# Where the sums of the two left-over keys stand in a unit's chain of sums: cross-attention and state-space kernel on one core

## The chip, the cores and the metric

The kernel runs on one core of one Trainium2 chip. The metric is the device time of one execution in microseconds (us), given as the median of the runs. The engines are TensorE (PE in the profile, its weight loads PEld), VectorE (DVE), ScalarE (ACT), GpSimd (POOL) and SyncE (SP, which issues DMAs).

## What is computed

The reference is one block of a sequence model, in float32, with batch 1, 4096 queries, 3202 keys, width 512, 8 heads of 64:

```
x  = layernorm(builder_state);  base_n = layernorm(base_state)      # 4096 x 512, 3202 x 512
x  = residual + mha(x, base_n)                                      # softmax attention, 8 heads
U  = (layernorm(x) @ W_in.T + b_in) @ Bmat                          # 4096 x 64
s  = silu(s @ A.T) + u_t   for t = 0 .. 4095                        # the scan
out = x + states @ Cmat + mean(program_probs) @ W_prog.T + b_prog
```

Softmax needs, for each query, the sum over 3202 keys of exp(score). The change concerns the order in which the parts of that sum are added up.

## The kernel before

**Preparation.** The keys and values are projected and written to DRAM, in chunks of 256 keys (12 chunks of 256, then one of 128: 3200 keys, `NDC` = 13 chunks with `c` = 0 to 12). The two keys that are left over (`REST` = 2) stay in SBUF tiles `kx` and `vx`.

**Units.** The attention runs over 64 units, numbered `i` = 0 to 63. A unit is a block of 512 queries (`Q` = 0 to 7), a pair of heads (`hp` = 0 to 3) and a half of the block's queries (`half`, 256 queries); the eight units of a block are 8Q to 8Q + 7. Each unit has, for each chunk `c`:

- `("scores", i, c)` on PE, line 635: eight matmuls of 64x256 into one of two PSUM tiles (ring `s`).
- `("weights", i, c)` on ACT, line 705: the exponential, 128x1024, into a tile `p`.
- `("product", i, c)` on PE, line 745: the weights times the values, accumulated in PSUM tile `po`. There is one `po` (ring `o`), so `("product", i, 0)` has to wait for `("join", i - 1)`.
- `("add", i, c)` for `c` = 1 to 12, line 713: a chain, the sum of the weights of all chunks into `acc`. The sums with `c` in `POOL_SUMS = (2, 6, 10)` run on POOL, the others on DVE. In the last unit all of them run on DVE.
- `("rest", i)` on DVE, line 699: two small sums that add the weights of the two left-over keys (tile `extra`) into rows of `acc`, on 2 partitions x 256 elements each.

After the last chunk come `("output", i)` (ACT, line 780: a copy of half of `po`), `("join", i)` (DVE, line 784: the other half of `po` added to it, which frees `po`), `("fold", i)` (POOL, line 720), `("sums", i)` (PE, line 763), `den` (ACT), `whole`, `inverse`, `scale` and `fall` (DVE, lines 801 to 811).

**Other work between the units.** Once in a half block PE has the output projection `("rows", Q, half, "outs")` of the block before (line 988, 16 matmuls of 128x512), and four times in a block the query projection `("heads", Q + 1, hp)` of the next block (line 312).

**The order.** Every one of these steps is a piece with an engine, an estimated cost, a due time, the pieces that it comes after, and slots of rings that it takes and gives back (`plan.add`). `Plan.order` (line 100) plays the pieces through with the estimated costs, each engine taking the ready piece that is due first, and the order that comes out is the order in which the instructions of every engine are written. On the chip each engine runs its instructions in that order and waits for semaphores. A changed dependence or cost of one piece therefore also changes the order of others.

In the chain of sums, `before` names the piece that a sum follows, and the `rest` piece is put in after `add` 1:

```python
before = {1: ("weights", i, 0), 2: ("rest", i)}.get(c, ("add", i, c - 1))
...
if c == 1:
    plan.add(("rest", i), "DVE", 1200, partial(rest, w), [("add", i, 1), ("extra", first)],
```

The chain of a unit is thus add 1 (DVE), rest (DVE), add 2 (POOL), add 3, 4, 5 (DVE), add 6 (POOL), add 7, 8, 9 (DVE), add 10 (POOL), add 11, 12 (DVE).

## Time and profile before

| | |
|---|---|
| time, median of 3 runs | 2006.42 us (2005.42 to 2007.58) |
| the profiled execution: its time | 2004.45 us |
| the profiled execution: span in the trace | 2002.6 us |
| PE busy | 1954.1 us (98%) |
| DVE busy | 1259.4 us (63%) |
| ACT busy | 1130.1 us (56%) |
| POOL busy | 789.5 us (39%) |
| mean granted PE clock | 0.995 |

A row of costly groups reads: line, engine, operation, output <- inputs, shapes, count, then total busy time and the mean time of one in ns, then the idle time of the engine just before these instructions and what ended it. A row of the waits reads: who waited, for whom, the total in us, how many times, the longest. A row of the timeline reads: start, duration, engine, line, operation, tiles, shape, count of the instructions that are merged in it, and in brackets the idle time before and its releaser. The row "windows" gives the busy time of engines in a stretch and the granted PE clock in it.

### The profile page before, as it was taken

The numbers are of one execution on the slowest core, as the hardware profiler recorded it, in microseconds if no ns is written. First come the engines' busy times: TensorE is split into PE (matmuls) and PEld (weight loads), VectorE is DVE, ScalarE is ACT, GpSimd is POOL, SyncE is SP. The second block draws the span as 40 slices with busy tenths as digits, with TensorE's granted clock in tenths as the row PEclk, the third lists the DMA queues.
The fourth block names the chain that finished last, engine by engine and source line by source line (L and its number), as shares of the span: only waits on it lengthen the run. The fifth ranks groups of instructions, "written<-read, shape, count | busy, mean of one in ns | idle before, by whom it ended". The sixth has DMA issues, their size and how long they took to land. (4 is left out here: it accounts for less than half of the span.)

```text
span 2002.6 us, 66617 instructions
## 1 busy us (share of the span) xinstructions
PE 1954.1 (98%) x29070; PEld 1251.4 (62%) x29070; DVE 1259.4 (63%) x1533; ACT 1130.1 (56%) x1478; POOL 789.5 (39%) x631
## 2 busy tenths in 40 slices
PE   8999999999999999999999999999999999999996
PEld 4444566666666666666666666666666666666764
DVE  4311367566866677667756785667766675667575
ACT  2233466566666566556656665666565666655552
POOL 2111234345533454245434543445334642444424
PEclk9999999999999999999999999999999999999998
DMA  5632323224332243123322332234322331444485
GB/s 173 192 100 66 101 80 97 58 79 111 106 79 79 82 112 92 59 81 90 107 65 79 106 107 73 79 95 113 86 78 59 101 92 52 148 142 144 129 207 182
DMA packets 246934, 204.28 MB, mean 102 GB/s; under 512 B 80808, under 2 KB 220072, under 8 KB 246636
## 3 DMA queue, kind: packets, MB, share of 16 engines
q1 hardware_dynamic: 242088, 192.28, 33.4%
q10 hardware_dynamic: 4548, 7.67, 1.2%
q8 instruction: 231, 3.78, 0.8%
q14 instruction: 67, 0.55, 0.1%
HBM read 156.32 MB, written 29.88 MB: 93 GB/s over the span
## 5 line engine op out<-in xcount | busy, mean ns | idle before, releaser
L705 ACT ACTIVATE p<-s,shifts 128x1024 f32<-128x1024 f32 (+1 forms) x832 | 883.2, 1080 | 559.7 <-PE s L635 540.0
L745 PE MATMUL po<-p,v 64*64 64x256 f32 x12800 | 822.6, 377 | 10.6 <-DVE o L784 10.6
L635 PE MATMUL s<-q,k 64*64 64x256 f32 x12800 | 826.5, 377 | 4.9 <-ACT p L705 3.9
L713 DVE TENSOR_TENSOR acc<-p,acc 128x1024 f32<-128x1024 f32 (+1 forms) x515 | 633.3, 1230 | 249.0 <-POOL acc L713 179.4
L713 POOL TENSOR_TENSOR acc<-p,acc 128x1024 f32<-128x1024 f32 x189 | 449.2, 2376 | 679.1 <-ACT p L705 362.2
L635 PEld LDWEIGHTS s<-q,k 64*64 64x64 f32 x12800 | 482.6, 133 | 233.3 <-ACT p L705 32.5
L745 PEld LDWEIGHTS po<-p,v 64*64 64x64 f32 x12800 | 487.8, 133 | 209.7 <-DVE o L784 15.2
L720 POOL TENSOR_TENSOR acc<-acc 128x512 f32<-128x512 f32 x64 | 91.5, 1430 | 160.9 <-DVE acc L713 153.3
L713 DVE TENSOR_TENSOR acc<-p,p 128x1024 f32<-128x1024 f32 x64 | 99.5, 1555 | 75.8 <-ACT p L705 70.2
L312 PE MATMUL pq<-xn,wq 128*128 128x512 f32 x256 | 118.3, 605 | 0.0
L804 DVE RECIPROCAL rd<-rd 128x256 f32<-128x256 f32 (+1 forms) x65 | 112.4, 1729 | 2.2
L988 PE MATMUL pa<-wo,o 128*128 128x512 f32 x240 | 107.0, 599 | 0.0
L699 DVE TENSOR_TENSOR acc<-x,acc 2x256 f32<-2x256 f32 x128 | 95.2, 744 | 2.5
L551 PE MATMUL pv<-wv,ct 128*128 128x512 f32 (+1 forms) x208 | 95.5, 611 | 1.0 <-ACT ct L519 0.7
L584 PE MATMUL pk<-ct,wk 128*128 128x512 f32 (+1 forms) x224 | 88.8, 549 | 0.0
L312 PEld LDWEIGHTS pq<-xn,wq 128*128 128x128 f32 x256 | 46.0, 189 | 57.6 <-issue 57.5
L784 DVE TENSOR_TENSOR o<-po,o 128x256 f32<-128x256 f32 x64 | 27.1, 423 | 84.3 <-ACT o L780 83.7
L988 PEld LDWEIGHTS pa<-wo,o 128*128 128x128 f32 x240 | 44.4, 190 | 56.0 <-issue 53.7
L321 ACT ACTIVATE q<-pq,bias 128x512 f32<-128x512 f32 x32 | 22.0, 687 | 98.4 <-PE pq L312 98.4
L519 DVE COPY ct<-tp_c 128x512 f32<-128x512 f32 (+1 forms) x13 | 8.5, 651 | 104.1 <-PE tp_c L283 104.1
L584 PEld LDWEIGHTS pk<-ct,wk 128*128 128x128 f32 x224 | 39.2, 190 | 42.6 <-issue 42.6
L551 PEld LDWEIGHTS pv<-wv,ct 128*128 128x128 f32 (+1 forms) x208 | 38.1, 192 | 44.3 <-issue 42.1
(215 smaller groups left out, 1200.3 us busy)
## 6 DMA issues: line engine op xcount, KB each, us to landing
k<-kd SPq DMA_DIRECT2D x432, 128.0 KB, 2.2
v<-vd SPq DMA_DIRECT2D x432, 128.0 KB, 2.3
xn<-x SPq DMA_DIRECT2D x416, 32.0 KB, 1.9
xr<-in_x_dram SPq DMA_DIRECT2D x30, 256.0 KB, 3.7
x1d<-xr SPq DMA_DIRECT2D x30, 256.0 KB, 3.4
x<-in_x_dram SPq DMA_DIRECT2D x28, 256.0 KB, 3.2
cx<-in_ctx_dram SPq DMA_DIRECT2D x25, 256.0 KB, 2.9
vd<-vs SPq DMA_DIRECT2D x25, 256.0 KB, 2.4
```

The costliest lines, as they stand in the source:

```text
L312: nc.tensor.matmul(pq, wq[:, i, hp * P : (hp + 1) * P], xn[:, i, :], start=(i == 0), stop=(i == NC - 1),)
L551: nc.tensor.matmul(pv[h * HD : h * HD + n, :H], ct[:, k, o : o + n], wv[:, k, :], start=(i == 0), stop=(i == NC // parts - 1), skip_group_ ...
L584: nc.tensor.matmul(pk[:, :n_g], wk[:, i, hp * P : (hp + 1) * P], ct[:, i, :n_g], start=(i == 0), stop=(i == NC - 1),)
L635: nc.tensor.matmul(s[k0 : k0 + HD, a, b, :], kts[(*w["at"][:2], c)][r, b * CK + k0 : b * CK + k0 + HD], q[r], start=True, stop=True, skip_ ...
L699: nc.vector.tensor_tensor(to[r], t[r], to[r], ALU.add)
L705: nc.scalar.activation(t[:, :, :nb, :], w["ps"][c][:, :, :nb, :], AF.Exp, bias=w["shift"])
L713: engine.tensor_tensor(w["acc"][:, :, :nb, :], t[:, :, :nb, :], before[:, :, :nb, :], ALU.add)
L720: nc.gpsimd.tensor_tensor(acc[:, :, 0, :], acc[:, :, 0, :], acc[:, :, 1, :], ALU.add)
L745: nc.tensor.matmul(w["po"][a * HD : (a + 1) * HD, k, :QU], vts[Q, hp, c][r, b, a * HD : (a + 1) * HD], t[r, a, b, :], start=(c == 0 and b ...
L784: nc.vector.tensor_tensor(o, rows_of(w, w["po"][:, 1, :QU], True), o, ALU.add)
L804: nc.vector.reciprocal(w["rd"][:, part], w["rd"][:, part])
L988: nc.tensor.matmul(v["pa"], o_t[Q, c, half][:, t * P : (t + 1) * P], wo[:, c, :], start=(c == 0), stop=(c == NC - 1),)
```

## The change

The two small sums stand after add 4 and before add 5, add 2 follows add 1 directly, and the planner's estimated cost of the `rest` piece is 900 ns in place of 1200 ns. The instructions are the same ones.

```diff
             if c:
                 dve = w["last"] or c not in POOL_SUMS
-                before = {1: ("weights", i, 0), 2: ("rest", i)}.get(c, ("add", i, c - 1))
+                before = {1: ("weights", i, 0), 5: ("rest", i)}.get(c, ("add", i, c - 1))
                 plan.add(("add", i, c), "DVE" if dve else "POOL", (100 + 1200 * part) if dve else 2382,
                          partial(add, w, c, nc.vector if dve else nc.gpsimd),
                          [("weights", i, c), before], d + 1200,
...
-            if c == 1:
-                plan.add(("rest", i), "DVE", 1200, partial(rest, w), [("add", i, 1), ("extra", first)],
+            if c == 4:
+                plan.add(("rest", i), "DVE", 900, partial(rest, w), [("add", i, 4), ("extra", first)],
                          d + 1300, [], [("extra", ("extra", first))])
```

## The prediction

> **What bounds the kernel now.** I read the page first, for the bound and the price of the moved work.

> ```profile
> PE 1954.1 (98%) x29070; PEld 1251.4 (62%) x29070; DVE 1259.4 (63%) x1533; ACT 1130.1 (56%) x1478; POOL 789.5 (39%) x631
> ...
> L699 DVE TENSOR_TENSOR acc<-x,acc 2x256 f32<-2x256 f32 x128 | 95.2, 744 | 2.5
> L784 DVE TENSOR_TENSOR o<-po,o 128x256 f32<-128x256 f32 x64 | 27.1, 423 | 84.3 <-ACT o L780 83.7
> ```

> PE is the bound; a small sum costs nothing by itself, whether it lies early or late, unless PE ends up waiting. The waits of PE say where that is. Its longest is for the join (L784), the one reader that frees the single `po`:

> ```profile
> PE po L745 <- DVE o L784: 10.6, 8, 2.6
> ```

> So I followed, unit by unit, the DVE queue ahead of each join in the timeline. Between units 10 and 11 the join is late, yet PE loses nothing:

> ```profile
> 506.43 2.63 DVE L713 TENSOR_TENSOR acc<-p,p 128x1024 f32<-128x1024 f32 x1 [0.96 <-ACT p L705]
> ...
> 508.98 1.94 DVE L713 TENSOR_TENSOR acc<-p,acc 128x1024 f32<-128x1024 f32 x2
> 509.14 1.91 PE L635 MATMUL s<-q,k 64*64 64x256 f32 x32
> ...
> 510.83 1.82 DVE L699 TENSOR_TENSOR acc<-x,acc 2x256 f32<-2x256 f32 x2
> ...
> 510.97 7.13 PE L988 MATMUL pa<-wo,o 128*128 128x512 f32 x16
> ...
> 512.68 0.42 DVE L784 TENSOR_TENSOR o<-po,o 128x256 f32<-128x256 f32 x1
> ```

> The rows are add 1 of unit 11, add 11 and 12 of unit 10, rest of unit 11, join of unit 10. The join ends at 513.10, and PE would have reached product 0 of unit 11 at 509.14 + 2 x 0.864 (a step of eight matmuls) = 510.87. The output projection (L988) stands between and covers it.

> Between units 50 and 51 the same projection stands three products later, and the join, held up by rest, stops PE for 1.3 us:

> ```profile
> 1583.86 1.91 PE L635 MATMUL s<-q,k 64*64 64x256 f32 x32
> ...
> 1584.60 1.80 DVE L699 TENSOR_TENSOR acc<-x,acc 2x256 f32<-2x256 f32 x2
> ...
> 1586.43 0.42 DVE L784 TENSOR_TENSOR o<-po,o 128x256 f32<-128x256 f32 x1
> ...
> 1586.91 0.88 PE L745 MATMUL po<-p,v 64*64 64x256 f32 x12 [1.15 <-DVE o L784]
> ```

> The last passage that matters lies between units 3 and 4. There add 2 of the new unit (POOL) meets add 11 and 12 of the old one (DVE):

> ```profile
> 323.69 3.99 DVE L713 TENSOR_TENSOR acc<-p,acc 128x1024 f32<-128x1024 f32 x2
> 323.81 3.32 POOL L713 TENSOR_TENSOR acc<-p,acc 128x1024 f32<-128x1024 f32 x1 [2.10 <-DVE acc L699]
> ...
> 327.60 0.41 DVE L784 TENSOR_TENSOR o<-po,o 128x256 f32<-128x256 f32 x1
> 328.07 4.51 PE L745 MATMUL po<-p,v 64*64 64x256 f32 x48 [2.63 <-DVE o L784]
> ```

> The two DVE sums take 3.99 us where they took 1.94 above, and POOL's takes 3.32 where its mean is 2376 ns: one engine's sum waits while the other's runs, and POOL's came in between DVE's two. (The passage at 1832.10, unit 59 to 60, gives 3.99 and 3.32 again.)

> **The change, part by part.**

> *The two sums themselves.* The same 128 instructions, 0.84 us a pair when undisturbed, 1.8 to 2.9 us where a POOL sum overlaps. Moved to after add 4, they delay add 5 by 0.84 us; the chain there has slack, because whole, inverse and scale wait for ACT (whole of unit 9 idles 0.79 us for it). I take 0; if that cover were gone, it would cost at most 64 x 0.84 = 54 us, which no row suggests.

> *Rest leaves the queue ahead of the join, and add 2 no longer waits for it.* The good side is where rest made PE wait. The bad side is that POOL starts add 2 right behind add 1, which is where DVE has add 11 and 12 of the old unit and then the join.

> *The planner's order.* I compared the order written for both kernels. PE keeps its 1956 pieces and its 138 changes between quarter and whole-array matmuls; 58 pieces move. In units 11, 19, 27, 35, 43 and 59 the projection goes from ahead of product 0 to behind product 2. In units 5, 13, 21, 29, 37 and 45 the query projection goes from ahead of product 0 to behind product 4. In units 3, 4 and 60 scores 6 goes behind product 1. So the planner takes away the covers, counting on early joins. In those same units POOL's add 2 now comes ahead of the old unit's fold. SP's queue keeps its order.

> *New stalls.* Where POOL's add 2 comes before DVE's add 12, I price the passage by the row at 323.69: the join ends 4.32 us after add 11 starts, PE goes on 0.06 later. Unit 11: 508.98 + 4.38 = 513.36 against 510.87, a stall of 2.5. By the same sum units 19, 27, 35, 43 give 2.4, 2.1, 2.4, 2.2; together 11.6. Units 13, 21, 29, 37, 45 give 1.17 each (unit 13: add 11 at 562.58, so 566.96 against 565.77), 5.9. Units 3, 5 and 59 give 1.1 each, 3.3. In all of them add 2's inputs are there before DVE ends add 11 (unit 13: weights 2 end at 563.09, add 11 at 563.79). Sum: +20.8. Bounds: if DVE's two sums run through first, the join of unit 10 would end at 511.36, a stall of 0.5, and those of the 13 kind vanish: +2.7 in all.

> *Stalls that go.* At units 12, 20, 28, 36, 44 PE now waits 1.2 to 1.3 for a join behind rest (unit 12: 542.30 instead of 541.08); 6.4 in all. After the change rest is gone from there and the old unit's chain is earlier (its add 6 moves ahead of POOL's other sums), as in units 51 to 52, where the wait is only 0.2. Unit 51: 1.3. Unit 4: 2.8 for the join, 0.6 for scores 6, and 1.7 for a slow stretch of the clock (below). Unit 60: 1.5 + 0.6. Unit 3: 0.55 for scores 6. Small ones (0.2 at unit 52, 0.17 at six units like 13, 0.3 at unit 58): 1.5. Sum: -17.0. What is late next is scores, bound by PE itself.

> *The clock.* After the 2.63 us of idle time at unit 4, PE ran at half speed for a while:

> ```profile
> 325.58:328.99 3.41, 0.92 (x17) 1.00 0.00 0
> 328.99:332.40 3.41, 3.41 (x38) 0.50 0.02 5
> 332.40:335.81 3.41, 3.41 (x68) 1.00 0.17 31
> ```

> (columns: stretch, its length, PE busy and count, granted clock, DMA share, GB/s). The price is half of 3.41, 1.7 us. Idle times of 1.15 (unit 51) and 1.31 (unit 60) left the clock at 1.00. The five new stalls of 2.1 to 2.5 lie between, nearer to 2.63 than to 1.31; whether one lowers the clock should hang on how it falls across these stretches of 3.41. I take two or three of five, +4.3, bounds 0 and 8.5.

> [...]

> *Sum.* 20.8 - 17.0 + 4.3 = +8.1 us on the profiled execution: 2004.45 becomes 2012.5. The median before stands 1.97 higher, so I forecast 2014.4 us.

> **The rivals.**

> 1. *The clock never drops* (2.5 is too short). +3.8 us, 2010.2. For it: 1.31 did nothing. Against it: 2.63 did. Chance 0.20.
> 2. *It drops at four or all five.* +10.6 to +12.3, up to 2018.7. Chance 0.10.
> 3. *The other sign: POOL does not get in.* If DVE's add 12 starts before POOL's waiting add 2, joins come early, new stalls are 2.7, and with the 17.0 saved the result is -14.3, 1992.1. The deciding point is who goes first when add 11 ends. Both passages that show it (323.69 and 1832.10) let POOL in. Chance 0.10.
> 4. *The saved stalls stay.* At units 12, 20, 28, 36, 44 the join now also stands behind add 11 and 12 of the old unit; if POOL's add 10 or the normalizing work on DVE delays these, the 6.4 come back: +14.5, 2020.9. Units 51 to 52 speak against it, in this order with a wait of 0.2. Chance 0.10.

> The forecast keeps 0.50.

> **How the numbers follow.** A measurement of this kernel can tell about 0.2%, 4 us, from no change. Faster by more (below 2002.4): rival 3 and a little for stalls that prove smaller, 0.12. Within it (2002.4 to 2010.4): most of rival 1, 0.15. Slower: the rest, 0.73. The range leaves out rival 3 and most of rival 4: from 2006, rival 1 with 4 us less of new stalls, to 2020, rival 2 with 1.3 for scatter of the runs.

> **What would show it.** Right: rows "PE po <- DVE o" with some 13 waits at the starts of units 3, 5, 11, 13, 19, ... of 2 and 1 us by turns, add 11 and 12 taking about 4 us on DVE there, no waits at units 12, 20, 28, and granted clock 0.50 behind some of the 2 us waits. Wrong: if the joins at units 11 and 13 end before PE is there, or if PE waits for something other than a join, such as scores for an `extra` that comes late.

## The result and the profile after

| | before | after |
|---|---|---|
| time, median (lowest to highest) of 6 runs each | 2005.64 us (2004.39 to 2007.58) | 2022.58 us (2021.07 to 2024.16) |
| the profiled execution: its time / its span | 2004.45 / 2002.6 us | 2022.41 / 2020.5 us |
| mean granted PE clock | 0.995 | 0.990 |

The changed kernel is slower: 1.0084 times the time before, interval 1.0071 to 1.0097. That is 17 us where the prediction had 8, and it lies above the range of 2006 to 2020.

The engines' row and the join's row of the page, and then what the trace has for the small sums (shortest, median and longest duration in ns, then the times of the first and the last):

```profile
PE 1960.7 (97%) x29070; PEld 1258.1 (62%) x29070; DVE 1244.7 (62%) x1533; ACT 1131.0 (56%) x1478; POOL 798.1 (40%) x631
...
L784 DVE TENSOR_TENSOR o<-po,o 128x256 f32<-128x256 f32 x64 | 26.9, 421 | 126.7 <-ACT o L780 126.7
```

```profile
L699 DVE TENSOR_TENSOR acc<-x,acc x128: 369/415/419, 233.7 to 1942.2; 2x256 f32<-2x256 f32 x128
```

The moved sums are cheaper than before: none takes more than 419 ns, where their mean was 744: none is held up beside a POOL sum any more. DVE as a whole does 15 us less. So the loss is not work. It is in the waits of PE, whose first row has doubled, while its count went from 8 to 13:

```profile
PE po L745 <- DVE o L784: 21.3, 13, 3.4
```

Below, a wait is counted as the prediction did it, from the time at which PE would have reached the product; that makes each 0.18 us longer than this row has it, and the 13 together 23.6.

Where the joins were late before, they are early now. The timeline between units 3 and 4, then between 50 and 51:

```profile
322.70 1.92 PE L635 MATMUL s<-q,k 64*64 64x256 f32 x32
...
323.77 0.43 DVE L784 TENSOR_TENSOR o<-po,o 128x256 f32<-128x256 f32 x1 [0.77 <-ACT o L780]
...
324.44 1.91 PE L745 MATMUL po<-p,v 64*64 64x256 f32 x32
```

```profile
1602.85 1.91 PE L635 MATMUL s<-q,k 64*64 64x256 f32 x32
1603.86 0.42 DVE L784 TENSOR_TENSOR o<-po,o 128x256 f32<-128x256 f32 x1 [0.37 <-ACT o L780]
...
1604.58 1.69 PE L745 MATMUL po<-p,v 64*64 64x256 f32 x28
```

In both the bracket says that DVE itself was idle ahead of the join, until ACT's `output`, and PE goes from scores to product without a gap. Between units 10 and 11 it went the other way:

```profile
506.68 2.41 DVE L713 TENSOR_TENSOR acc<-p,p 128x1024 f32<-128x1024 f32 x1 [1.18 <-ACT p L705]
...
509.01 3.98 DVE L713 TENSOR_TENSOR acc<-p,acc 128x1024 f32<-128x1024 f32 x2
...
509.23 3.21 POOL L713 TENSOR_TENSOR acc<-p,acc 128x1024 f32<-128x1024 f32 x1 [1.22 <-DVE acc L713]
...
509.39 1.91 PE L635 MATMUL s<-q,k 64*64 64x256 f32 x32
...
512.91 0.41 DVE L784 TENSOR_TENSOR o<-po,o 128x256 f32<-128x256 f32 x1
...
513.38 1.10 PE L745 MATMUL po<-p,v 64*64 64x256 f32 x8 [2.08 <-DVE o L784]
```

Add 2 of the new unit (POOL, 509.23) starts while DVE is in add 11 of the old one, and gets in ahead of add 12: DVE needs 3.98 us for two sums. The output projection is gone from behind the scores. PE would have reached the product at 511.12 (509.39 + 2 x 0.864) and starts it at 513.38, right behind the join, 2.26 us later. What this does to the clock (stretch, length, then busy time and count of PE, PEld, DVE, ACT and POOL, granted clock, DMA share, GB/s):

```profile
349.62:353.03 3.41, 2.77 (x28) 1.67 (x32) 3.31 (x4) 0.00 (x0) 1.27 (x1) 0.50 0.02 5
510.05:513.46 3.41, 1.33 (x28) 0.65 (x24) 3.38 (x4) 2.43 (x4) 2.78 (x2) 1.00 0.57 173
513.46:516.88 3.42, 3.42 (x36) 2.06 (x40) 2.96 (x2) 0.00 (x0) 0.87 (x1) 0.50 0.23 74
```

Half speed (granted clock 0.50) follows at once on the wait at unit 11, and so it does at units 19, 27, 35 and 43 (from 731.91, 950.37, 1168.82 and 1387.27) and behind unit 5 (from 349.62). Before, one stretch within the attention was at half speed; now six are.

The time from scores 3 of one unit to scores 3 of the next, after minus before, places the whole difference (us):

| units | difference |
|---|---|
| 11, 19, 27, 35, 43 | +20.3 (4.00 to 4.19 each) |
| 13, 21, 29, 37, 45 | +5.1 |
| 5 | +4.8 |
| 3, 52, 53, 58, 59 | +2.9 |
| 12, 20, 28, 36, 44 | -6.7 |
| 4 | -5.2 |
| 51, 56, 60 | -3.9 |
| sum over units 2 to 60 (small units included) | +17.3 |

The spans differ by 17.9.

### The profile page after: what moved, and what is told of

The parts are those of the page before. It is cut to its first block, busy times and chain, and to the rows that moved or that the text cites. A ratio compares the mean times of both kernels' runs of the same rounds, so it can differ in the third digit from the quotient of the medians.

```text
span 2020.5 us, 66641 instructions
## 1 busy us (share of the span) xinstructions
PE 1960.7 (97%) x29070; PEld 1258.1 (62%) x29070; DVE 1244.7 (62%) x1533; ACT 1131.0 (56%) x1478; POOL 798.1 (40%) x631
## 5 line engine op out<-in xcount | busy, mean ns | idle before, releaser
L705 ACT ACTIVATE p<-s,shifts 128x1024 f32<-128x1024 f32 (+1 forms) x832 | 884.0, 1080 | 565.5 <-PE s L635 553.1
L745 PE MATMUL po<-p,v 64*64 64x256 f32 x12800 | 832.5, 380 | 21.3 <-DVE o L784 21.3
L635 PE MATMUL s<-q,k 64*64 64x256 f32 x12800 | 828.8, 378 | 3.7 <-ACT p L705 2.7
L713 DVE TENSOR_TENSOR acc<-p,acc 128x1024 f32<-128x1024 f32 (+1 forms) x515 | 661.8, 1285 | 248.1 <-POOL acc L713 175.1
L713 POOL TENSOR_TENSOR acc<-p,acc 128x1024 f32<-128x1024 f32 x189 | 455.9, 2413 | 793.0 <-ACT p L705 400.9
L745 PEld LDWEIGHTS po<-p,v 64*64 64x64 f32 x12800 | 494.0, 134 | 217.3 <-DVE o L784 27.2
L635 PEld LDWEIGHTS s<-q,k 64*64 64x64 f32 x12800 | 483.0, 133 | 232.5 <-issue 28.7
L713 DVE TENSOR_TENSOR acc<-p,p 128x1024 f32<-128x1024 f32 x64 | 92.8, 1450 | 69.0 <-ACT p L705 63.4
L988 PE MATMUL pa<-wo,o 128*128 128x512 f32 x240 | 107.0, 599 | 0.0
L784 DVE TENSOR_TENSOR o<-po,o 128x256 f32<-128x256 f32 x64 | 26.9, 421 | 126.7 <-ACT o L780 126.7
L988 PEld LDWEIGHTS pa<-wo,o 128*128 128x128 f32 x240 | 44.4, 190 | 56.0 <-issue 55.6
L982 POOL TENSOR_TENSOR xr<-xr,rowb 128x512 f32<-128x512 f32 x30 | 52.7, 1767 | 22.3 <-DMA xr<-in_x_dram 15.8
```

What stands on the lines that cost most here:

```text
L635: nc.tensor.matmul(s[k0 : k0 + HD, a, b, :], kts[(*w["at"][:2], c)][r, b * CK + k0 : b * CK + k0 + HD], q[r], start=True, stop=True, skip_ ...
L705: nc.scalar.activation(t[:, :, :nb, :], w["ps"][c][:, :, :nb, :], AF.Exp, bias=w["shift"])
L713: engine.tensor_tensor(w["acc"][:, :, :nb, :], t[:, :, :nb, :], before[:, :, :nb, :], ALU.add)
L745: nc.tensor.matmul(w["po"][a * HD : (a + 1) * HD, k, :QU], vts[Q, hp, c][r, b, a * HD : (a + 1) * HD], t[r, a, b, :], start=(c == 0 and b ...
L784: nc.vector.tensor_tensor(o, rows_of(w, w["po"][:, 1, :QU], True), o, ALU.add)
L982: nc.gpsimd.tensor_tensor(v["x"], v["x"], rowb, ALU.add)
```

## The experiments

The theory (A): the place of the small sums costs PE nothing. What costs is the planner's new order, in which POOL's add 2 gets in ahead of DVE's add 12, so that the join is late, where the projections no longer cover it; half speed follows. The rival (B): the late place itself costs, through the chain that now waits in other places.

All kernels but one take the finished list of pieces and move some of them; nothing is planned anew. `shift(out, names, behind)` takes the named pieces out of the list and puts them back right behind another piece. Ratios are to the kernel before, run beside them on the same chip. It measured 2006.8 beside `e1` to `e4`, 2005.9 beside `e5` to `e9` and 2005.6 beside `e10` and `e11`, so times of different groups compare to about 1 us.

### The move alone, and the order alone

`e1_rest_alone` keeps the order of before and moves nothing but the small sums:

```diff
+    for i in range(64):
+        shift(out, [("rest", i)], ("add", i, 4))
```

> The kernel before with its planned order kept on every engine, and only the two small sums of each unit issued later on DVE, behind add 4. Theory A (joins held up by POOL's add 2 where the planner took the cover away, and the clock that drops behind the long ones): PE keeps its covers, so no new waits at units 11, 13 and the like; the waits at units 12, 20, 28, 36, 44 and 51 go (7.7 us), units 4 and 60 lose 0.8 each and unit 4 perhaps its clock drop (1.7): about 1995.5 us, 1993 to 1999. Theory B (the sums cost time where they now stand, in the middle of the chain, whatever PE's order is): about as slow as the changed kernel, 2020 to 2024.

Measured 1996.34 us, 0.995 (0.9934 to 0.9967). `e2_order_alone` is the opposite: the changed kernel's order, with the small sums put back to their old place.

```diff
+    for i in range(64):
+        shift(out, [("rest", i)], ("add", i, 1))
```

> The changed kernel with its planned order kept on every engine, and only the two small sums issued where they were before, behind add 1. Theory A: the covers are gone and rest is ahead of the joins as well; waits of 2.5 to 3.3 us at units 11, 19, 27, 35, 43 with clock drops, 1.2 to 2 at unit 13 and the like: 2022 to 2035 us. Theory B: the sums are back, so about 2006 us.

Measured 2046.32 us, 1.0199 (1.0182 to 1.0216), 11 us above the upper end of what was expected. The rows of PE's waits for the join, first in `e1_rest_alone`, then in `e2_order_alone`:

```profile
PE po L758 <- DVE o L797: 1.9, 2, 1.6
```

```profile
PE po L758 <- DVE o L797: 34.9, 15, 3.2
```

| | sums behind add 1 | sums behind add 4 |
|---|---|---|
| order of before | 2005.6 (before) | 1996.3 (`e1_rest_alone`) |
| new order | 2046.3 (`e2_order_alone`) | 2022.6 (after) |

In either order the move saves time, 9 us and 24 us; in either place the new order costs, 41 us and 26 us. B falls. In `e2_order_alone` the waits are 13.6 us more than after, and nine stretches instead of six are at half speed (5.1 us at 1.7); that is 18.7 of the 23.1 between the profiled executions. The rest is spread thin (mostly 0.25 in each of units 12, 20, 28, 36, 44 and 52, 1.4 in units 60 and 61 together, 1.3 in the tail), and its causes are not known.

### Is it POOL's add 2 that makes the join late?

`e3_fold_first` puts add 2 of the new unit behind add 12 of the old one again, where the new order had it ahead of the old unit's fold (14 places):

```diff
+    for i in range(1, 64):
+        names = [p["name"] for p in out]
+        if i < 63 and names.index(("add", i, 2)) < names.index(("fold", i - 1)):
+            shift(out, [("fold", i - 1), ("add", i, 2)], ("add", i - 1, 12))
```

> The changed kernel with POOL's fold of the old unit and then add 2 of the new one behind the old unit's add 12, in the units where the planner put add 2 ahead of fold; nothing else moves, PE's covers stay away. Theory A: POOL no longer gets in between DVE's add 11 and 12, so the join comes 2 us earlier; waits of 0.5 at units 11, 19, 27, 35, 43, none at 13, 21, 29, 37, 45, 1.4 at unit 5, no clock drops in mid kernel: 2022.6 - 19.7 - 10.2 = about 1993 us, 1990 to 1998. Rival (the order of PE alone does it, whatever POOL does): stays at 2018 or above.

Measured 1996.82 us, 0.9952 (0.9936 to 0.9969): 25.8 us below after, by moving two pieces of POOL at each of 14 places. Its row of waits, and then its timeline between units 10 and 11:

```profile
PE po L760 <- DVE o L799: 1.2, 3, 0.8
```

```profile
506.63 1.94 DVE L728 TENSOR_TENSOR acc<-p,acc 128x1024 f32<-128x1024 f32 x2
...
506.76 1.91 PE L650 MATMUL s<-q,k 64*64 64x256 f32 x32
...
508.49 0.41 DVE L799 TENSOR_TENSOR o<-po,o 128x256 f32<-128x256 f32 x1
...
508.96 1.96 PE L760 MATMUL po<-p,v 64*64 64x256 f32 x32 [0.29 <-DVE o L799]
```

DVE's two sums take 1.94 us, not 3.98, and PE waits 0.29, not 2.08. The projection is still away from here: what remains of the wait without POOL is the 0.5 that the prediction gave as the lower bound. No stretch in mid kernel is at half speed.

`e8_rest_fold_first` asks whether the same helps at the two waits left in `e1_rest_alone`:

```diff
     for i in range(64):
         shift(out, [("rest", i)], ("add", i, 4))
+    for i in (4, 60):
+        shift(out, [("fold", i - 1), ("add", i, 2)], ("add", i - 1, 12))
```

> The kernel of the first experiment (planned order of before, small sums behind add 4) and in units 4 and 60 POOL's fold of the old unit ahead of add 2 of the new one. Theory A: the wait at unit 4 falls from 1.8 to 0 or 0.3 and at unit 60 from 0.5 to 0: about 1994 us, 1992 to 1996, faster than both kernels by 12 and 28 us.

Measured 1996.35 us, 0.9948 (0.9932 to 0.9965), the same as `e1_rest_alone`. The two waits are gone, but the 1.9 us saved at unit 4 are lost again in unit 5, where 2.2 are added: there PE has a small piece that prepares the exponents of the next unit (`spread` of unit 6) and waits for a DVE piece, `maximum`, that stands behind the sums. This `spread` comes 18.20 us behind scores 3 of unit 5 instead of 15.99.

### What the covers are worth

`e4_scores6_ahead` leaves the join late and gives PE scores 6 to do meanwhile, in the five units with the long waits:

```diff
+    for i in (11, 19, 27, 35, 43):
+        shift(out, [("product", i, 0), ("product", i, 1)], ("scores", i, 6))
```

> The changed kernel with scores 6 issued ahead of product 0 and 1 on PE in units 11, 19, 27, 35 and 43, a partial cover of 0.86 us. If the clock drops follow from the length of the idle time: the waits fall from 2.3 to about 1.5 and the clock stays at 1.00 behind them: 5 x (0.8 + 1.7) less, about 2010 us. If the clock drops come from something else, only the 4 us of the waits go: about 2018.5 us.

Measured 2009.21 us, 1.0014 (1.0005 to 1.0024). The five waits fell from about 2.35 to 0.78 to 1.08, at the price of 0.55 for scores 6 in each, so 0.9 us each is saved on waits; no half-speed stretch is left behind them. Five times 0.9 and five times 1.7 for the clock are 13.0 of the 13.4 that the kernel gained on after: two thirds of the gain are clock, although most of the idle time was only broken up.

`e9_outs_cover` moves the output projection back ahead of product 0 in the same units:

```diff
+    for Q, i in enumerate((11, 19, 27, 35, 43)):
+        shift(out, [("rows", Q, 1, "outs")], ("scores", i, 5))
```

> The changed kernel with the output projection issued ahead of product 0 again in units 11, 19, 27, 35 and 43, everything else as changed (the query projection stays late). Theory A: the five waits of 2.3 to 2.6 are covered (11.9 us) and the five clock drops behind them go (8.5 us): 2022.6 - 20.4 = about 2002 us, 2000 to 2005, although POOL still gets in between add 11 and 12. If the clock drops come with the change in another way: 2008 to 2011 us.

Measured 2006.47 us, 1.0 (0.9991 to 1.001). The five waits and their half-speed stretches are gone, 16 us; that is 4 us less than expected, since PE's `spread` now waits 0.63 in each of the five blocks for a `maximum` that stands behind add 7 on DVE, and the tail was 1.3 longer.

`e11_heads_cover` moves the query projection back in the five units with the 1.2 us waits. It was meant to show also whether the half-speed stretches go when a block's length changes:

```diff
+    for Q, i in enumerate((13, 21, 29, 37, 45)):
+        shift(out, [("heads", Q + 2, 0)], ("scores", i, 5))
```

> The changed kernel with the query projection issued ahead of product 0 again in units 13, 21, 29, 37 and 45; the output projection stays late. The five waits of 1.2 us are covered: 5.9 us less, and the five waits of 2.3 to 2.6 stay. If the clock drops behind these depend on how a wait falls across free-running stretches of 3.413 us: a block now takes 217.3 us with a drop, which is no whole number of stretches (63.7; it was 218.45, 64.0), so each block falls 1.2 us elsewhere and only two to four of the five drops are left in the profile: 2012 to 2015 us. If the length of the wait alone decides, all five stay: about 2016.7 us.

Measured 2022.68 us, 1.008 (1.0063 to 1.0097), no change against after. The five waits are covered (their row falls from 21.3 to 16.1), but a later step of the same unit, scores 10, now waits 1.06. A block stays 218.45 us long and all five half-speed stretches stay, so the question of the block's length was not tested.

### The small sums, and unit 5

`e5_no_small_sums` is the changed kernel without the two small sums, so two keys are missing from the denominators:

```diff
-        for k in range(2):
-            r, to = slice(k * HD, k * HD + REST), w["acc"][:, :, 0, k * P : (k + 1) * P]
-            nc.vector.tensor_tensor(to[r], t[r], to[r], ALU.add)
+        pass
```

> The changed kernel without the 128 small sums at all (they are left out, so the denominators miss the two left-over keys); the planned order is kept. Theory A: the sums cost nothing where the change puts them, so all waits and clock drops stay: 2022.6 us within 1.5. Theory B (the sums lengthen the chain in its middle): faster by a good part of the 17 us.

Measured 2017.08 us, 1.0057 (1.0041 to 1.0074). I had expected no change. Twelve of the thirteen waits are there as before (2.2 to 2.5 and 1.1 to 1.2 us); unit 5's is 1.63 instead of 3.59, with no half speed behind it. The rest is clock: its profile has two half-speed stretches instead of six. How much clock it saves differs from run to run: two runs took 2014.3 and 2014.7 us at a mean clock of 0.993 and 0.994 (the second is the profiled one), two took 2019.5 and 2020.0 at 0.991 and 0.990, so the median of 5.5 us below after stands for neither pair. Unit 27's wait had half speed behind it in after and has none here; PE was busy in its stretch for 1.46 us, a little longer than in the five of after that half speed followed (1.20 to 1.33 us):

```profile
943.13:946.54 3.41, 1.46 (x28) 1.00 0.50 150
946.54:949.96 3.42, 3.42 (x47) 1.00 0.54 155
```

(columns: stretch, length, PE busy and count, granted clock of that stretch, DMA share, GB/s; the second row shows full speed behind 1.46 us of busy time). So the waits of PE that come from the sums are in one unit of 64. That unit's timeline, in after:

```profile
342.30 1.23 DVE L713 TENSOR_TENSOR acc<-p,p 128x1024 f32<-128x1024 f32 x1
...
342.48 5.59 POOL L713 TENSOR_TENSOR acc<-p,acc 128x1024 f32<-128x1024 f32 x2 [6.70 <-DVE acc L713]
...
345.79 4.09 DVE L713 TENSOR_TENSOR acc<-p,acc 128x1024 f32<-128x1024 f32 x2 [2.26 <-POOL acc L713]
...
349.79 0.42 DVE L784 TENSOR_TENSOR o<-po,o 128x256 f32<-128x256 f32 x1
...
350.26 1.13 PE L745 MATMUL po<-p,v 64*64 64x256 f32 x8 [3.41 <-DVE o L784]
```

The first row is add 1 of unit 5, which DVE takes right behind add 9 of unit 4. POOL's add 10 of unit 4 is free to start with the end of add 9, and has to wait for it; when it is done, add 2 of unit 5 is ready too and follows at once, so the two take 5.59 us together. Add 11 starts only behind add 10, and loses to add 2 as elsewhere.

Two edits looked for what lets add 1 in there. `e6_unit5_add8` takes work of unit 3 out of DVE's way, so that add 9 would be earlier:

```diff
+    shift(out, [("whole", 3), ("inverse", 3, 0), ("scale", 3, 0), ("fall", 3)], ("add", 4, 8))
```

> The changed kernel with the four DVE steps whole, inverse, scale and fall of unit 3 issued behind add 8 of unit 4, as before, instead of ahead of it. Theory A: add 10 on POOL then no longer meets add 1 of unit 5, the wait at unit 5 falls from 3.6 to 1.1 and the clock drop behind it goes: 4.2 us less, about 2018.4 us (2017 to 2020). If the wait at unit 5 has another cause: 2022.6 us.

Measured 2023.48 us, 1.0084 (1.0068 to 1.0101): a miss. Add 10 still met add 1, POOL's two sums took 5.52, and the wait was 3.59 as before. `e10_unit5_add1_late` takes away the meeting itself:

```diff
+    shift(out, [("add", 5, 1), ("add", 5, 2)], ("join", 4))
```

> The changed kernel with add 1 of unit 5 issued on DVE behind add 11, add 12 and the join of unit 4, all other orders as changed. Theory (the sixth experiment left the wait at unit 5 as it was: without the long wait at unit 4, ACT is ahead, add 1's inputs are there early, DVE takes it right behind add 9 and POOL's add 10 has to wait, then add 2 follows it at once): now add 10 comes first, the join ends near 347.2, the wait at unit 5 falls from 3.6 to about 0.6 and no clock drop follows it: 4.7 us less, about 2017.9 us (2014 to 2020). If the wait has another cause: 2022.6 us.

Measured 2020.42 us, 1.0072 (1.0055 to 1.0089). POOL's two sums in that kernel stand apart, at their normal length:

```profile
342.70 2.37 POOL L725 TENSOR_TENSOR acc<-p,acc 128x1024 f32<-128x1024 f32 x1 [6.71 <-DVE acc L725]
...
348.73 2.38 POOL L725 TENSOR_TENSOR acc<-p,acc 128x1024 f32<-128x1024 f32 x1 [3.67 <-DVE acc L725]
```

Unit 5's wait is 0.61 and no half speed follows it, so POOL's two sums are its cause. This edit takes away two things at once, the meeting of add 10 with add 1 and the place of add 2 ahead of add 12. `e5_no_small_sums` tells them apart: there add 10 starts at 340.47, ahead of add 1 (342.20), and only add 2 still gets in ahead of add 12, and the wait is 1.63. So about 2.0 of the 3.59 come from the meeting and 1.0 from add 2. Of the 3 us, 2.04 came back later in the unit, where scores 10 waits for work of unit 6. This kernel also gave a price for the clock in one and the same passage: from scores 3 of unit 11 to scores 3 of unit 12 it takes 32.59 us with no half speed, where after takes 34.17 with it. The waits are 2.36 and 2.26; with them taken out the difference is 1.68.

## Why the prediction was wrong, point by point

*Right:* the direction (slower); that the sums by themselves make PE wait nowhere (unit 5 apart); the mechanism of the join (POOL gets in between add 11 and add 12, and the cover is gone), which `e3_fold_first` shows; the units in which it happens; and the sizes: 11.9 us at units 11, 19, 27, 35, 43 (11.6 in the prediction), 5.9 at 13, 21, 29, 37, 45 (5.9), about 1.1 each at units 3 and 59. The stalls that were to go did: -15.8 in the rows of units 4, 12 to 44, 51, 56 and 60 of the table, against -17.0, part of which was for small waits in other rows. Rival 3 (POOL does not get in) and rival 4 (the saved stalls stay) did not happen. The windows rule out rival 1 (the clock never drops). Of the prediction's readings, one was off without harm: POOL's add 2 now comes ahead of the old unit's fold in units 3, 5, 11, 13, 19, 21, 27, 29, 35, 37, 43, 45, 53 and 59; in units 4 and 60, which the prediction counts among them, it did so before and no longer does. Two slips of its arithmetic are as small: the lower bound of 2.7 takes unit 11's 0.55 for all five units (their own rows give 1.9), and 2006.42 plus 8.1 is 2014.5.

*The term that failed first: the clock.* I took two or three of five stretches at half speed, 4.3 us. All five came, 8.5, as rival 2 had it at a chance of 0.10; its 2018.7 would still have been in the range. A sixth came behind unit 5, 1.7. Together that is 5.9 more than forecast. I treated the five as separate throws. In this kernel they are not: the stretches of half speed begin 218.4 to 218.5 us apart, which is 64.0 stretches of 3.413, so each of the five waits falls at the same place of a stretch. In `e10_unit5_add1_late` the wait of unit 11 fell across two stretches and cost no clock (2.19 and 2.46 us busy, granted clock 1.00 in both), while those of units 19 to 43 cost some. In `e5_no_small_sums` the stretch from 943.13 (above) ends 218.45 us behind the start of the half-speed one at 728.09, so again at the same place, and full speed followed it (1.46 us busy). That a half-speed stretch in each block holds the next wait in place is argued from these spacings, and no run shows it by itself. What the traces show is a count: in after, `e5`, `e6`, `e10` and `e11` a long wait whose block before had dropped the clock dropped it too in 15 of 16 cases. It is no rule of all or none, since `e10` has four of five and the profile of `e5` two. The forecast should have had all five as the likeliest count, not as one end of the range.

*The second: unit 5's wait*, taken at 1.1 as for units 3 and 59, measured 3.59. I priced it by the rows of another unit and did not see that unit 4, no longer held up for 5 us, has the inputs of the next unit's add 1 ready earlier. In the kernel before, add 1 of unit 5 waited 3.74 us for its weights from ACT and started at 346.79, when POOL's add 10 (343.19 to 345.56) was done; now it starts right behind add 9, ahead of add 10. This is 2.5 more.

*A third, small:* PE waits 1.2 us more for a DMA of `xn` in unit 58. By the waits' rows it is between 0.5 and 2.3 in the kernels run here (1.1 before, 2.3 after, which is the longest), with no relation to their edits that I can see. Each has one trace, so that it is scatter, and not the change, is not shown.

8.1 of the forecast, 5.9 for the clock, 2.5 for unit 5, 0.3 for the other new waits and 1.2 for the DMA are 18.0; the profiled executions differ by 17.96. That it closes so well is partly luck: the new waits (23.6), the clock (10.2) and the DMA (1.2) less the 17.3 of the table leave 17.7 for the stalls that went, not 17.0, and 0.7 were added outside the units. What the change was worth without the planner's answer to it is in `e1_rest_alone`: 9 us faster than before. That kernel, `e8_rest_fold_first` and `e3_fold_first` are the best found, 1.3% below after.

## What to carry to other kernels

Where a planner writes the order, a moved dependence is two changes: the move, and the order that the planner makes of it. Run each alone before judging either; here one was worth -9 us and the other +26. A wait that comes back in every block at the same place of a clock stretch should not be priced as so many separate throws: here 15 of 16 waits whose block before had lost clock lost it again. And where the sums of two engines hold each other up, as here (3.98 us for DVE's two beside 1.94), the question is which of them goes next (POOL's, in all 14 units), not only how long each takes.

## What the hardware did that I had not expected

```profile
568.42:571.84 3.42, 1.43 (x29) 1.00 0.45 139
571.84:575.25 3.41, 3.41 (x40) 0.50 0.25 77
346.56:349.97 3.41, 1.44 (x28) 1.00 0.36 113
349.97:353.39 3.42, 2.73 (x52) 1.00 0.15 41
```

```profile
507.11:510.52 3.41, 2.19 (x44) 1.00 0.36 89
510.52:513.94 3.42, 2.46 (x48) 1.00 0.49 155
725.57:728.98 3.41, 1.23 (x24) 1.00 0.66 196
728.98:732.40 3.42, 3.42 (x36) 0.50 0.48 140
```

In the attention (unit 0 to the last join) of before and after, the stretches that half speed followed had 0.64 to 1.33 us busy, and all others 1.82 or more. Three rows from other runs lie between: 1.43 (`e2_order_alone`) was followed by half speed, 1.44 (the same run) and 1.46 (`e5_no_small_sums`) were not. Outside the attention it went otherwise: in the kernel before, 2.16 us busy from 21.79 and 1.46 from 1987.87 were followed by half speed too. So busy time is not the whole rule, and the ends of matmuls are modelled in these records. In the second fence the same 2.4 us wait does no harm at unit 11, where it is split over two stretches (2.19 and 2.46 us busy), and costs 1.7 us at unit 19, where it lies in one (1.23 us busy). In after, 2.1 us of idle time (2.08 in the row at 513.38 above) were enough.

*POOL's waiting sum went next.* When DVE's add 11 ended, POOL's waiting add 2 began before DVE's add 12, although DVE had that queued right behind: 3.98 us for two DVE sums in place of 1.94. So it went in all 14 units of the changed kernel in which add 2 stands ahead of the old fold: add 11 and 12 take 3.97 to 4.09 us there (in unit 5 add 2 goes ahead of add 11 already). Between units 10 and 11 add 11 runs from 509.01 to 510.22, and add 12, on record from 510.26, takes 2.73 us and ends at 512.99, 0.55 behind POOL's add 2. Both engines lost by it: 3.98 and 3.21 us beside 1.94 and 2.37. That POOL's sum goes first is read from these times; what decides it, no run shows.
